# Statistics matmuls in a free column of the column transform's bank, and mixing pieces and head steps behind layer 3 dealt anew

## The chip, the cores and the metric

The kernel runs on one core of one Trainium2 chip. The metric is the device time of one execution in microseconds (us); lower is better. Runs are compared by their medians.

The engines are called by the profile's names: PE is the matmul engine (PEld its weight loads), DVE the vector engine, ACT the activation engine, POOL and SP the two that issue DMAs here. Results of matmuls land in PSUM, the accumulation memory, whose unit is a bank of 512 fp32 columns.

## The reference: what is computed

Eight images of 8 channels in 4 groups, 256 x 256 pixels each, go through two residual stages:

```python
x = x + _L0_conv_ref(_gn(x), ...)     # a spectral network
x = x + _L1_conv_ref(_gn(x))          # 3x3 dilation
```

`_gn` takes mean and variance of every group of an image and normalises by them. The spectral network lifts each group to 10 channels (fc0), and then four layers follow, each the sum of a spectral convolution (2D FFT, 12 x 12 low modes at two corners mixed by weights, inverse FFT) and of a 1x1 convolution. After each of the first three layers stands a gated activation. A head (fc1 to 128 channels per group, the activation, fc2 back to 2 channels per group) ends the network. The dilation is a 3x3 maximum with a border of -2; it needs mean and variance of the *whole* finished first stage before it can scale its result.

## The kernel before, in words

**Tiling.** An image's state `h` stays in SBUF as 11 chunks (`NCH`). Transforms are matmuls with cosine and sine tables; all is fp32.

**PSUM.** All eight banks are taken by two kinds of tiles: `ps_a` (L59) gives one bank, kind "one", two buffers; `ps_tri` (L62) gives three banks, kind "tri", two buffers. `ps_four` (L65) takes one of each, which makes four banks. A new tile of a kind goes to the older of the two buffers, and its first writer waits until the last reader of the tile there has ended.

**Order of the work.** PE, DVE, ACT and SP run in the order in which the program writes their instructions (`tc.manual_schedule`, L919). The order is dealt by hand: the generator `layers` (L691) writes image b's four layers and yields short strings, and for each letter the loop at L926 puts in other work:

- "f" is `first()` (L803), an f step: fc1 for a block of pixels of the image before, 4 products into a `ps_four` (8 matmul rows in the trace, L813), then two activations on ACT (L814, L815). A head has 128, f0 to f127. Every third or so first issues a load of `hs`, the stored state, on SP (`load_state`, L784).
- "c" is `second()` (L818), a c step: fc2 for two f steps (16 matmul rows, L830) into a "one" tile `acc`, which DVE then adds to `y` (L837 or L839). A head has 64, c0 to c63. With "c" the add is written at once; with "C" it is left until the next "f" or "c".
- "t" is `tail()` (L914), one step of the dilation of the image whose head has ended (`dilate`, L859).

Besides, layer 3 calls `next(side)` (L502, L612, L615), and each call writes one piece of the *next* image's preparation, the generator `start` (L673): `spectrum_x` (L265: its statistics and spectrum), then `mix` for layer 0 (L403: twelve pieces n0 to n11 on DVE, L411 and L414 in turn, the sums `fs` L432, and the folding matmuls `p_f`, L455 and L464, with DVE copies after them). What is left of it when layer 3 is over is written by `rest` (L680), between groups of head steps that the table `REST` (L43) lists:

```python
REST = ("ff", "f", "f", "fC", "fc"), ("f", "fc", "ffC", "ff", "fc")
...
        for n, _ in enumerate(then):
            yield REST[b > 0][n]
            for _ in range(2 if b == 0 else 1):
                if c < NCH:
                    read_x(b + 1, c)
                    c += 1
```

The first list is for image 0, the second for the others. `read_x(b + 1, c)` (L529) issues four SP DMAs that bring chunk c of the next image into `h`; behind image 0 all eleven are issued in `rest`, behind the others chunks 7 to 10 (chunks 0 to 6 are issued in layer 3, L621).

Counting the letters: the head of image b-1 ends (c63) in the `rest` behind image b, where f0 and on of image b's own head begin. Behind images 1 to 6 the order before is, with the last pieces of layer 3 in front,

```
burst 10, f126, c62, n4 n5, n6 n7, read 6 | n8 | f127 | read 7 | n9 | f0 c63 | read 8 | n10 |
f1 f2 C0 | read 9 | n11 | f3 f4 | read 10 | fs | f5 c1 | p_f and copies | f6 f7 c2 | p_g ...
```

**The finished image's statistics.** The tail begins with `stats_end` (L223). It joins the collected moments (L225, DVE), sums the means over a group's partitions by a matmul with `grp` (L229), takes them off (L231 to L234, DVE), sums the variances by a second matmul (L238) and ends in a reciprocal root on DVE (L242 and `rsqrt`, L248). Both matmuls have one output column, and each takes a "tri" tile of its own. The tail's first call lies in layer 0 of the image after (b = 2 to 7); the third lies behind `transform(0)` there, and the fifth behind `transform(1)`. The tail of image 6 and that of image 7 run in the drain at the end of the program (L946 to L953).

**The column transform.** `transform(k)` (L548), in layers 0 to 2: 64 matmuls (L558) into a `ps_four` named `p_d`, of which at most 480 of each bank's 512 columns are used; then DVE copies the "one" bank (L561) and ACT the three others (L562). In layer 0 there follow on PE a `burst` (L580, tiles `p_z`, L587 and L593, ended by ACT at L598) and, two steps later, `gather` (L564).

Of the kernel before, what the change touches and what calls it, by code (L numbers as in the profile page):

```python
# [13 lines left out]
ALU = mybir.AluOpType  # L14
# [25 lines left out]
DR = 2  # L40
STEPS = 128
BEHIND = mybir.DependencyInfo(mybir.DependencyClass.Sync, mybir.DependencyReason.DATA)
REST = ("ff", "f", "f", "fC", "fc"), ("f", "fc", "ffC", "ff", "fc")  # L43


@with_exitstack
def fno_dilate_kernel(ctx: ExitStack, tc: tile.TileContext, a: dict, out: bass.AP):
# [14 lines left out]
    def ps_tri(name):  # L62
        return ps.tile([128, 3, 512], F32, tag="tri", bufs=2, name=name)
# [5 lines left out]
    def part(i):  # L69
        return slice(32 * i, 32 * i + 32)  # L70
# [139 lines left out]
    def copy_banks(pairs, by_act):  # L210

        done = []
        for i, (dst, src) in enumerate(pairs):
# [6 lines left out]
                    tc.declare_no_dep(ins, other, reason="two engines read banks of one tile and write apart")  # L220
            done.append(ins)

    def stats_end(st, name, out_):  # L223
        mv = sb.tile([128, 2], F32, tag="mv", name=f"mv_{name}")
        nc.vector.bn_aggr(mv, st.rearrange("p n s -> p (n s)"))  # L225
        yield
        yield
        p = ps_tri(f"p_st_{name}")[:, 0, :]
        mm(p[:, 0:1], grp, mv[:, 0:1], start=True, stop=True)  # L229
        mr = sb.tile([128, 2], F32, tag="mr", bufs=4, name=f"mr_{name}")  # L230
        nc.vector.tensor_copy(mr[:, 0:1], p[:, 0:1])  # L231
        d = sb.tile([128, 1], F32, tag="d", name=f"d_{name}")
        nc.vector.tensor_tensor(d, mv[:, 0:1], mr[:, 0:1], ALU.subtract)
        nc.vector.scalar_tensor_tensor(mv[:, 1:2], d, d, mv[:, 1:2], ALU.mult, ALU.add)  # L234
        yield
        yield
        q = ps_tri(f"p_sv_{name}")[:, 0, :]
        mm(q[:, 0:1], grp, mv[:, 1:2], start=True, stop=True)  # L238


        v, r = mv[:, 0:1], mr[:, 1:2]
        nc.vector.tensor_scalar(v, q[:, 0:1], EPS, None, ALU.add)  # L242
        rsqrt(v, r, d)
        yield
        out_["mr"] = mr
# [19 lines left out]
    def spectrum_x(b, out_):  # L265

        x = turned[:, 0:2].rearrange("p i (g f) -> p i g f", g=G)
        st = sb.tile([128, G, 2, 6], F32, tag="bn", bufs=1, name=f"bn_x{b}")
        for i in range(2):
            for g in range(G):  # L270
                nc.vector.bn_stats(st[:, g, i, :], x[:, i, g])
            yield
        mv = sb.tile([128, G, 2], F32, tag="mvx", name=f"mv_x{b}")
        for g in range(G):
            nc.vector.bn_aggr(mv[:, g], st[:, g].rearrange("p n s -> p (n s)"))
        yield
        yield
        yield
        p = ps_a(f"p_st_x{b}")
        group_means(p, mv[:, :, 0])  # L280
        mr = sb.tile([128, 2, G + 1], F32, tag="mrx", name=f"mr_x{b}")
        d = sb.tile([128, 2, G + 1], F32, tag="dx", bufs=1, name=f"d_x{b}")
        nc.vector.tensor_copy(mr[:, 0], p[:, : G + 1])
        dm = d[:, 0, :G]
        nc.vector.tensor_tensor(dm, mv[:, :, 0], mr[:, 0, :G], ALU.subtract)
        nc.vector.tensor_tensor(dm, dm, dm, ALU.mult)
        nc.vector.tensor_tensor(dm, dm, mv[:, :, 1], ALU.add)
        yield
        yield
        q = ps_a(f"p_sv_x{b}")  # L290
        group_means(q, dm)
        nc.vector.tensor_scalar(d[:, 1], q[:, : G + 1], EPS, None, ALU.add)
        rsqrt(d[:, 1], mr[:, 1], d[:, 0])
        out_["mr"] = mr[:, :, G]
        for g in range(G):
            nc.vector.tensor_scalar(
                x[:, :, g], x[:, :, g], mr[:, 0, g : g + 1], mr[:, 1, g : g + 1], ALU.subtract, ALU.mult)
            if g != 1:
                yield
        yield  # L300

        a1, a2 = turned[:, 2, 0:512], turned[:, 2, 512:1024]
        a3 = turned[:, 2, 1024:1216].rearrange("p (g m) -> p g m", g=G)
        nc.vector.memset(a3, 0.0)
        p = ps_a(f"p_a1_{b}")
        for i in range(2):
            for g in range(G):
                mm(p[part(g)], er[:, i, :], x[:, i, g], start=i == 0, stop=i == 1)
        nc.vector.tensor_copy(a1, p)
        yield  # L310
        yield
        t = ps_a(f"p_a2_{b}")
        for i in range(4):
            nc.tensor.transpose(t[:, 128 * i : 128 * (i + 1)], a1[:, 128 * i : 128 * (i + 1)], ident)
        nc.vector.tensor_copy(a2, t)
        yield
        yield
        p = ps_a(f"p_a3_{b}")
        for j in range(2):
            for i in range(2):  # L320
                mm(p[:, 24 * j : 24 * j + 24], a2[:, 256 * j + 128 * i : 256 * j + 128 * i + 128], fw[:, i, 0:24],
                   start=i == 0, stop=i == 1)
        for g in range(G):
            nc.vector.tensor_copy(a3[part(g), g, :], p[part(g), 0:48])
        yield
        yield
        cols = a3.rearrange("p g (j k) -> p g j k", j=2)
        p = ps_a(f"p_xs_{b}")
        for k in range(2):
            for term in range(2):  # L330
                for q in range(4):
                    k0 = 12 * term + 3 * q
                    mm(p[part(q), 24 * k : 24 * k + 24], unf[:, spectrum_table(k, term), :],
                       cols[:, :, :, k0 : k0 + 3], start=term == 0, stop=term == 1)
        xe4 = xe.rearrange("p (s k) g j -> p s g j k", s=2)
        for k in range(2):
            nc.vector.tensor_copy(
                xe4[:, k, :, 0:2, :],
                p[:, 24 * k : 24 * k + 24].rearrange("p (g j k) -> p g j k", g=G, j=2),
            )  # L340
        yield
        bt = sb.tile([128, 2, 3, G, WID], F32, tag="B", bufs=1, name=f"B_{b}_0")
        prod = turned[:, 0, :1200].rearrange("p (i g o j) -> p i g o j", i=6, g=G, o=WID)
        for i in range(6):
            nc.vector.tensor_tensor(
                prod[:, i], wext, xe[:, i].unsqueeze(2).to_broadcast([128, G, WID, 5]), ALU.mult
            )
        nc.vector.tensor_reduce(
            bt.rearrange("p s k g o -> p (s k g o)"),
            prod.rearrange("p i g o j -> p (i g o) j"), AX.X, ALU.add,  # L350
        )
        out_["bt"] = bt
        yield
        yield

    def spectrum_table(k, term):

# [45 lines left out]
    def mix(b, l, out_):  # L403
# [3 lines left out]
        for n in range(12):  # L407
            k, k2 = n // 4, n // 2 % 2
            pr = turned[:, 2, 1024 * k2 : 1024 * k2 + 800].rearrange("p (g m i) -> p g m i", g=G, i=WID)
            if n % 2 == 0:  # L410
                nc.vector.tensor_tensor(  # L411
                    pr, sw[k], bt[:, k2, k].unsqueeze(2).to_broadcast([128, G, 2 * WID, WID]), ALU.mult)
            else:
                nc.vector.tensor_reduce(  # L414
                    s[k2][:, k].rearrange("p s o g -> p (s o) g"),
                    pr.rearrange("p g m i -> p m g i"), AX.X, ALU.add,
                )
            if l == 0:
                if n % 2 or n > 7:
                    yield  # L420
            elif n not in (0, 2, 6, 10):
                yield {1: "fc", 4: "fC", 7: "fC", 9: "fC"}.get(n, "f")
            if n == 2 and l == 3 and b + 1 < n_img:
                load_x(b + 1)
# [109 lines left out]
    def layer(b, l, out_, stored, side, ahead):  # L534
# [13 lines left out]
        def transform(k):  # L548


            cs = chunks_of(k)
            n, lo = len(cs), cs[0] % 3
            step = cs[-1] % 3 - lo if n == 2 else 1
            t = turned[:, lo : lo + step * (n - 1) + 1 : step].rearrange("p n (r v i) -> p n r v i", r=2 * NQ, v=8)
            one, tri, banks = ps_four(f"p_d_{b}_{l}_{k}")
            for v in range(8):
                for q in range(NQ):
                    mm(banks[q][part(v % 4), : 240 * n], fw8[part(q), v, :],  # L558
                       t[part(q), :, :, v, : NBLK * WID], start=v < 4, stop=v >= 4)
            e = turned[:, (2 * k + 1) % 3, : 960 * n].rearrange("p (q x) -> p q x", q=NQ)  # L560
            nc.vector.tensor_copy(e[:, 0], one[:, : 240 * n])  # L561
            nc.scalar.activation(e[:, 1:4], tri[:, :, : 240 * n], AF.Identity)  # L562
# [116 lines left out]

    def rest(b, then):  # L680
        c = 0 if b == 0 else NCH - 4
        for n, _ in enumerate(then):
            yield REST[b > 0][n]
            for _ in range(2 if b == 0 else 1):
                if c < NCH:
                    read_x(b + 1, c)
                    c += 1
        for i in range(c, NCH):
            read_x(b + 1, i)

    def layers(b, stored, d, then, ahead):  # L691

# [431 lines left out]
```

## Time and profile before

| what | us |
|---|---|
| median of 3 runs (3689.13 to 3691.84) | 3690.49 |
| the profiled execution | 3688.73 |
| its span, first to last instruction | 3687.0 |
| PE busy in the span | 3486.2 |
| ACT busy | 2865.0 |
| DVE busy | 2386.8 |
| from one `p_f` (L464) to the next, images 1 to 7 | 433.4, 438.7, 439.5, 436.8, 437.8, 438.5 |

The times in the table's upper part come from runs without and with the profiler; the rows below belong to the profiled execution alone. In the timelines, a row is a run of like instructions: start, length, engine, line, output and inputs, the count, and in brackets how long the engine had been idle before and what ended that. The ends of matmuls are modelled, so the start of the next row is the safer mark. Matmul rows count two for each fp32 product.

### The profile page before, as it was taken

To read this page: it belongs to the slowest core of one execution; us is meant where nothing else is said; L and a number is where in the kernel's file an instruction comes from. 1 tells how busy PE (TensorE), PEld (TensorE's weight loads), DVE (VectorE), ACT (ScalarE), POOL (GpSimd) and SP (SyncE) were. 2 spreads that over 40 slices of the span, in tenths; PEclk is the share of its full clock that TensorE was granted. 3 is DMA by queue.
4 is the path that set the end of the run, shared out by engine and by line. 5 is a ranking of instruction groups with operands and counts; after the bars stand their busy time and mean duration, and the time that the engine had idled before them with its cause. 6 is when DMAs were issued, how large, how long until landed. Compare 5 with 4: busy or idle time off the path is not lost.

```text
span 3687.0 us, 112658 instructions
## 1 busy us (share of the span) xinstructions
PE 3486.2 (95%) x50872; PEld 1270.1 (34%) x50872; DVE 2386.8 (65%) x3711; ACT 2865.0 (78%) x3021; POOL 117.1 (3%) x202
## 2 busy tenths in 40 slices
PE   5768999999999999999999999999999999999997
PEld 2323333333333333333333333333333333333222
DVE  6776666557775677757776577765777567772443
ACT  2436888888788788787888888888888888889986
POOL 1000000000000000000000000000000000000000
PEclk7879999999999999999999999999999999999998
DMA  3005111532226212271224512253222521225221
GB/s 92 16 17 212 49 50 46 165 106 72 72 84 195 68 58 72 87 226 53 65 57 138 170 55 75 64 168 114 67 73 89 189 75 58 71 65 193 84 82 48
DMA packets 114080, 344.71 MB, mean 93 GB/s; under 512 B 15984, under 2 KB 18480, under 8 KB 98176
## 3 DMA queue, kind: packets, MB, share of 16 engines
q1 hardware_dynamic: 95392, 276.32, 24.5%
q0 software_dynamic: 18208, 61.18, 5.1%
q8 instruction: 400, 6.55, 0.7%
q14 instruction: 80, 0.66, 0.1%
HBM read 213.44 MB, written 123.74 MB: 91 GB/s over the span
## 4 chain that ended last, share of the span: by engine, by line
PE 73%; DVE 16%; issue 5%; ACT 4%; DMA 2%; POOL 0%; ACTq 0%; DVEq 0%; POOLq 0%
PE p_fc L830 20%; PE p_fc L813 19%; PE p_z L593 9%; PE p_d L558 7%; PE p_z L590 7%; PE p_z L587 3%; DVE y L839 3%; PE p_u L572 3%; DVE turned L541 3%; DVE S L414 3%; DVE turned L411 2%; DMA yin<-y_rows 2%; DVE turned L372 1%; PE p_b L381 1%; PE p_g L509 1%
## 5 line engine op out<-in xcount | busy, mean ns | idle before, releaser
L815 ACT ACTIVATE act<-p_fc 128x1536 f32<-128x1536 f32 x1024 | 1493.2, 1458 | 0.0
L813 PE MATMUL p_fc<-hs,c_w 32*128 32x512 f32 x8192 | 1133.4, 625 | 41.2 <-DVE y L839 20.8
L830 PE MATMUL p_fc<-act,c_w 128*32 128x512 f32 x8192 | 1007.0, 600 | 0.2 <-ACT act L815 0.2
L814 ACT ACTIVATE act<-p_fc 128x512 f32<-128x512 f32 x1024 | 616.6, 602 | 228.2 <-PE p_fc L813 216.8
L541 DVE STREAM_TRANSPOSE turned<-h 128x1024 f32<-128x1024 f32 x528 | 632.6, 1226 | 189.7 <-ACT h L598 189.0
L598 ACT ACTIVATE h<-p_z 128x512 f32<-128x512 f32 (+1 forms) x528 | 511.9, 1021 | 213.9 <-PE p_z L593 213.9
L839 DVE TENSOR_TENSOR y<-p_fc,y 128x512 f32<-128x512 f32 x392 | 267.9, 684 | 539.1 <-PE p_fc L830 539.1
L813 PEld LDWEIGHTS p_fc<-hs,c_w 32*128 32x128 f32 x8192 | 358.3, 183 | 613.4 <-ACT act L814 253.3
L830 PEld LDWEIGHTS p_fc<-act,c_w 128*32 128x32 f32 x8192 | 221.4, 109 | 703.9 <-issue 330.8
L593 PE MATMUL p_z<-c_binv,zt 32*128 32x256 f32 x5632 | 410.3, 405 | 0.0
L590 PE MATMUL p_z<-h,c_wt 32*32 32x512 f32 x8448 | 357.8, 601 | 7.9 <-ACT act L814 4.2
L593 PEld LDWEIGHTS p_z<-c_binv,zt 32*128 32x128 f32 x5632 | 258.9, 186 | 308.0 <-issue 295.1
L558 PE MATMUL p_d<-turned,c_fw 32*32 32x480 f32 (+1 forms) x9216 | 307.6, 539 | 0.6 <-DVE turned L541 0.2
L562 ACT ACTIVATE turned<-p_d 128x1440 f32<-128x1440 f32 x144 | 183.0, 1271 | 89.5 <-PE p_d L558 86.3
L600 ACT ACTIVATE h<-p_z,c_bias 128x512 f32<-128x512 f32 (+1 forms) x176 | 186.4, 1110 | 72.0 <-PE p_z L593 71.8
L215 ACT ACTIVATE zt<-p_g 128x198 f32<-128x198 f32 (+2 forms) x118 | 53.4, 575 | 182.7 <-PE p_g L487 99.9
L414 DVE TENSOR_REDUCE S<-turned 128x80 f32<-128x800 f32 x192 | 189.0, 984 | 5.9
L411 DVE TENSOR_TENSOR turned<-t,B 128x800 f32<-128x800 f32 x192 | 188.7, 983 | 0.9
L558 PEld LDWEIGHTS p_d<-turned,c_fw 32*32 32x32 f32 x9216 | 127.1, 103 | 165.6 <-issue 64.7
L372 DVE STREAM_TRANSPOSE turned<-zt 128x960 f32<-128x960 f32 x96 | 176.8, 1867 | 2.5
L590 PEld LDWEIGHTS p_z<-h,c_wt 32*32 32x32 f32 x8448 | 92.9, 103 | 175.3 <-DVE y L839 48.8
L572 PE MATMUL p_u<-turned,c_stack 128*32 128x480 f32 (+1 forms) x1152 | 136.7, 543 | 11.5 <-DVE turned L561 6.2
(192 smaller groups left out, 1763.1 us busy)
## 6 DMA issues: line engine op xcount, KB each, us to landing
stored<-h SPq DMA_DIRECT2D x88, 1024.0 KB
hs<-stored SPq DMA_DIRECT2D x352, 256.0 KB
t<-in_spw SPq DMA_DIRECT2D x96, 400.0 KB
yin<-y_rows POOLq DMA_DIRECT2D x56, 512.0 KB, 5.2
h<-in_xp SPq DMA_DIRECT2D x352, 48.0 KB
turned<-in_xw SPq DMA_DIRECT2D x16, 1024.0 KB
y<-in_x SPq DMA_DIRECT2D x56, 256.0 KB
y_rows<-y POOLq DMA_DIRECT2D x56, 256.0 KB, 4.0
```

Source lines behind the costliest of these rows:

```text
L411: nc.vector.tensor_tensor(pr, sw[k], bt[:, k2, k].unsqueeze(2).to_broadcast([128, G, 2 * WID, WID]), ALU.mult)
L414: nc.vector.tensor_reduce(s[k2][:, k].rearrange("p s o g -> p (s o) g"), pr.rearrange("p g m i -> p m g i"), AX.X, ALU.add,)
L541: nc.vector.transpose(dst[:, 2 * i : 2 * i + 2], h[:, c, 2 * i : 2 * i + 2].rearrange("p f (s x) -> p f s x", s=2))
L558: mm(banks[q][part(v % 4), : 240 * n], fw8[part(q), v, :], t[part(q), :, :, v, : NBLK * WID], start=v < 4, stop=v >= 4)
L590: mm(o, wt[part(q), l, g, :], h[part(q), c, f, :], start=True, stop=False)
L593: mm(banks[q][:, HW * s : HW * (s + 1)], zt[part(q), 2 * c + s].rearrange("p f o -> p (f o)"), binv[part(q), :], start=False, stop=s == 1)
L598: nc.scalar.activation(dst, src, AF.Silu)
L813: mm(banks[g], w1[part(g), blk, :], hs[k][part(g), :], start=True, stop=True)
L814: nc.scalar.activation(act[:, 0, :], one, AF.Silu)
L815: nc.scalar.activation(act[:, 1:4, :], tri, AF.Silu)
L830: mm(acc[part(g), :], w2[:, g, 15 - rb - i : 47 - rb - i], act[:, g, :], start=i == 0, stop=i == 1)
L839: nc.vector.tensor_tensor(y, sums, y, ALU.add)
```

## The change

It has two parts.

**The statistics matmuls.** In layer 0, `transform(0)` and `transform(1)` now call `tail()` themselves, between their matmuls and the copies L561 and L562, if a tail is waiting. During that call the transform's "one" tile is set as `guest`, and `stats_end` puts its matmul's single column into column 511 of that tile, in place of a "tri" tile. Two added yields in `stats_end` make up for the two added calls, so the DVE instructions of the tail stay at the calls at which they stood.

**Dealing.** `spectrum_x` loses one of two yields at its end, and layer 0's `mix` yields after every second piece to the end, not after every piece from n8 on. That leaves three calls for `rest` in place of six. `REST` has three groups for each list, and four chunks are read per group. The order behind images 1 to 6 becomes

```
burst 8, ..., f123, n0 n1 | burst 9, f124, c61, n2 n3, f125, n4 n5 | burst 10, f126, c62, n6 n7, n8 n9, read 6 |
f127 f0 c63 | reads 7 8 9 10 | n10 n11 | f1 f2 | fs | C0 f3 f4 c1 f5 | p_f and copies | f6 f7 c2 | p_g ...
```

where before n0 to n3 stood with burst 9 and n4 to n7 with burst 10. Behind image 0 the head steps keep their order (f0 to f4, C0, f5, c1), and the reads are dealt 4, 4, 3 in place of 2, 2, 2, 2, 2, 1. Behind image 7 `rest` returns at once.

```diff
-REST = ("ff", "f", "f", "fC", "fc"), ("f", "fc", "ffC", "ff", "fc")
+REST = ("fff", "ff", "Cfc"), ("ffc", "ff", "Cffcf")
...
+    guest = [None]
+
+    def corner(name):
+
+        return ps_tri(name)[:, 0, 0:1] if guest[0] is None else guest[0][:, 511:512]
+
     def stats_end(st, name, out_):
...
-        p = ps_tri(f"p_st_{name}")[:, 0, :]
-        mm(p[:, 0:1], grp, mv[:, 0:1], start=True, stop=True)
+        p = corner(f"p_st_{name}")
+        mm(p, grp, mv[:, 0:1], start=True, stop=True)
+        if guest[0] is not None:
+            yield
         mr = sb.tile([128, 2], F32, tag="mr", bufs=4, name=f"mr_{name}")
-        nc.vector.tensor_copy(mr[:, 0:1], p[:, 0:1])
+        nc.vector.tensor_copy(mr[:, 0:1], p)
...
-        q = ps_tri(f"p_sv_{name}")[:, 0, :]
-        mm(q[:, 0:1], grp, mv[:, 1:2], start=True, stop=True)
+        q = corner(f"p_sv_{name}")
+        mm(q, grp, mv[:, 1:2], start=True, stop=True)
+        if guest[0] is not None:
+            yield
...
-        nc.vector.tensor_scalar(v, q[:, 0:1], EPS, None, ALU.add)
+        nc.vector.tensor_scalar(v, q, EPS, None, ALU.add)
...
         out_["bt"] = bt
         yield
-        yield
...
             if l == 0:
-                if n % 2 or n > 7:
+                if n % 2:
                     yield
...
+            if l == 0 and k < 2 and tails:
+                guest[0] = one
+                tail()
+                guest[0] = None
             e = turned[:, (2 * k + 1) % 3, : 960 * n].rearrange("p (q x) -> p q x", q=NQ)
...
     def rest(b, then):
         c = 0 if b == 0 else NCH - 4
-        for n, _ in enumerate(then):
+        if b + 1 == n_img:
+            return
+        for n in range(3):
             yield REST[b > 0][n]
-            for _ in range(2 if b == 0 else 1):
-                if c < NCH:
-                    read_x(b + 1, c)
-                    c += 1
-        for i in range(c, NCH):
-            read_x(b + 1, i)
+            for i in range(c + 4 * n, min(c + 4 * n + 4, NCH)):
+                read_x(b + 1, i)
+            next(then, None)
```

## The prediction, on record before the result

> **What bounds the kernel now.** I read the page first:
>
> ```profile
> PE 3486.2 (95%) x50872; PEld 1270.1 (34%) x50872; DVE 2386.8 (65%) x3711; ACT 2865.0 (78%) x3021; POOL 117.1 (3%) x202
> ...
> PE 73%; DVE 16%; issue 5%; ACT 4%; DMA 2%; POOL 0%; ACTq 0%; DVEq 0%; POOLq 0%
> ```
>
> PE is busy 95% of the span and holds 73% of the chain that ended last; most of its idle 200 us lie in image 0's stretch, ahead of 340 us. So a gain has to be taken out of PE's own timeline: rows that vanish, and gaps or stretched rows. I therefore read PE's timeline at the two places that the diff touches. Behind layer 3 of image 1 (f127 starts at 760.30):
>
> ```profile
> 760.30 2.47 PE L813 MATMUL p_fc<-hs,c_w 32*128 32x512 f32 x16
> ...
> 764.56 1.14 PE L813 MATMUL p_fc<-hs,c_w 32*128 32x512 f32 x8
> 767.51 1.14 PE L813 MATMUL p_fc<-hs,c_w 32*128 32x512 f32 x8 [1.81 <-DVE y L839]
> ...
> 770.43 2.93 PE L813 MATMUL p_fc<-hs,c_w 32*128 32x512 f32 x18
> 773.58 1.13 PE L813 MATMUL p_fc<-hs,c_w 32*128 32x512 f32 x6 [0.22 <-ACT act L815]
> ...
> 776.50 0.88 PE L455 MATMUL p_f<-fs,c_fold 32*32 32x72 f32 x64
> ...
> 781.49 0.73 PE L487 MATMUL p_g<-c_rowg,fz 32*128 32x264 f32 x8
> ```
>
> The reader is to see two losses. f2 waits 1.81 us for the add of c63. And f3, f4, f5 stand in a row: 24 matmul rows take 770.43 to 774.64, 4.21 us, where three free groups of eight take 3 x 1.07 = 3.21 (764.56 to 765.63 is one). DVE's timeline says why f2 waits: c63 ended on PE at 764.56, but two mixing pieces written ahead of its add were still in DVE's queue:
>
> ```profile
> 764.85 0.98 DVE L411 TENSOR_TENSOR turned<-t,B 128x800 f32<-128x800 f32 x1
> 765.87 0.99 DVE L414 TENSOR_REDUCE S<-turned 128x80 f32<-128x800 f32 x1
> 766.77 0.68 DVE L839 TENSOR_TENSOR y<-p_fc,y 128x512 f32<-128x512 f32 x1
> ```
>
> The 1.81 recurs behind images 2 to 6. The second place is `transform(0)` in layer 0, in image 2 with a tail and in image 1 without one:
>
> ```profile
> 798.79 2.24 PE L558 MATMUL p_d<-turned,c_fw 32*32 32x480 f32 x64
> 800.96 0.38 PE L229 MATMUL p_st_y<-mv_y,c_grp 128*128 128x1 f32 x2
> 801.27 1.74 PE L587 MATMUL p_z<-h,wcn 6*32 6x512 f32 x32
> 802.95 1.15 PE L593 MATMUL p_z<-c_binv,zt 32*128 32x256 f32 x16
> ...
> 365.38 2.19 PE L558 MATMUL p_d<-turned,c_fw 32*32 32x480 f32 x61
> ...
> 368.61 1.15 PE L593 MATMUL p_z<-c_binv,zt 32*128 32x256 f32 x16
> ```
>
> From the start of the transform to the burst's L593 it takes 4.16 us with the statistics and 3.23 without: 0.93. The same for `transform(1)`: 812.23 to 816.43 against 377.88 to 381.16, 4.20 against 3.28, 0.92. Only 0.31 of it is the matmul itself (800.96 to 801.27); the rest is the burst, whose L587 rows are stretched to 1.74, since the small matmul's "tri" tile turned the rotation: the burst's three banks are now those that the transform has just filled, and ACT's copy of them (L562) takes 1.37 us. The granted clock was 1.00 in both stretches.
>
> **What the skill says.** PSUM — Partial Sum Buffer, Specifications: eight banks of 512 fp32 values per partition; the kernel's tiles take all eight, so a statistics matmul can only borrow. The trace agrees as far as it shows the burst wait. The same page, "PSUM bank collisions raise a hardware error": a matmul must not write a bank and quadrant that another engine reads, so that accesses are to be guarded by bank. Here it means that the copy L561 has to come after the statistics matmul; no run here shows a collision. TensorE: Matmul & The Clock Gate, Part 1: the clock is set to 4/8 after a slack window of about 3.4 us. The trace agrees: behind image 1 it has stretches of 3.41 us at half clock, at 1206.1 (3 us after such a 1.81 wait) and at 1230.0.
>
> **The change part by part.** *Statistics matmuls* (images 2 to 7, six times). Removed: two "tri" tiles per image, thus the turned rotation. The burst then takes the three banks of the burst before, which ACT frees at 800.82 (798.88 + 1.94), before PE wants them. Remaining: the matmul, 0.31 each. So 0.93 + 0.92 - 2 x 0.31 = **1.2 us per image**. Bounds: 0.9, if the 128-row matmul cannot begin under the transform's tail as the burst's first rows do now (367.01 against 367.45), to 1.3. Added waits: the copy L561 stands behind the matmul, 0.3 us later; behind it on DVE are the tail's three short operations and two transposes, and DVE then idles 1.49 us, so nobody is late. If that cover went, the cost would be 0.3. The "one" bank stays taken until L231 (801.67) or L242 (815.15); its next users are f12 at 803.91 and f15 at 817.40. The matmul waits for L225, done at 788.1. POOL's DMAs of the tail stand at the same calls. Images 1 and 0 have no tail there, and the drain's two tails take the old way: nothing.
>
> *Dealing, behind images 1 to 6.* Four pieces, n6 to n9, lie on DVE from 761.01 to 764.85, then c63's add at once: it ends at 765.54, where it ended at 767.45. f1 ends at 765.63, so f2's wait is gone. I follow PE on: f2 to 766.70; C0 needs f1's activation, which ends at 767.66, halfway through it: to 768.65; f3 to 769.72; f4 needs the add of C0, on DVE behind n10, n11 and `fs` (766.2 + 1.94 + 0.87 = 769.0, then 0.75): 0.1 wait, to 770.88; c1 to 772.73 (1.85); f5 to 773.80; `p_f` to 775.0 (1.21); f6 waits for f5's activation, some 0.1, then f6, f7 and c2 (2.14 + 1.85, with 0.1 for that wait) to 779.1. `p_g` stood at 781.49: **2.3 us per image**. Of it 1.85 is the add and the rest is c1 between f4 and f5, so that ACT, which takes 1.82 per f step (759.65 to 761.46), isn't fed three in a row. Bounds: below, 0.9, if ACT falls behind at f5 to f7 and only half of the wait is kept; above 2.9, the bare sum of the rows.
>
> The pieces that come earlier, n0 to n5, go into DVE's idle time ahead of the adds of c61 and c62 (2.45 us and 1.71 us idle there): n0 and n1 end at 753.7, and c61 is due at 754.17; n2 to n5 run 754.78 to 758.7, and c62 is due at 760.41. Nothing, while that cover holds; without it up to 1.9 per pair of pieces. Their data (`sw`, `bt`) were there at 751.7.
>
> *Reads.* SP takes them in this order before:
>
> ```profile
> 760.48 5.23 SPq L532 DMA_DIRECT2D h<-in_xp  x8
> 766.49 0.35 SPq L789 DMA_DIRECT2D hs<-stored  x1
> 767.07 4.89 SPq L532 DMA_DIRECT2D h<-in_xp  x8
> 772.30 0.35 SPq L789 DMA_DIRECT2D hs<-stored  x1
> ```
>
> After, state 3 (f0) goes ahead of read 7, and reads 7 to 10, 16 issues at some 0.63, stand ahead of state 4 (f3): at about 774, 2 us later. It is first used by f12 at 803.9. Read 10 waits for chunk 10's store, issued at 759.79, and comes at about 771. Chunks 7 to 10 are read by bursts after 820. Nothing. POOL's queue gets c63's row write 1.9 earlier, and its first `yin` load with it. Behind image 0 the head steps and SP's order (state 3, reads 0 to 3, state 4, the rest) are the same, and DVE's pieces run without a break in both: nothing.
>
> Sum: 6 x 1.2 + 6 x 2.3 = 7.2 + 13.8 = 21.0. Span 3687.0 - 21.0 = 3666.0; profiled execution 3667.7; the median of the runs stands 1.8 above it: **3669.5**.
>
> **Rivals.** *A, both parts as worked*: 3669.5; with the upper bounds of both, 6 x 4.2 = 25, it is 3665; downward it reaches halfway to B, 3674. *B, ACT takes the wait's place*: after the dealing f1 to f7 come closer together, and ACT has 1.82 of every f step. For it: f127 and f0 are already stretched (2.47 for two). Against: nine f steps are 16.4 us of ACT in about 19 of PE. Then the dealing gives 0.9 and the sum is 6 x 2.1 = 12.6: 3678. *C, the dealing gives nothing*, for another add becomes as late as c63's was, or the program's order isn't what I counted: 6 x 1.1: 3684. *D, slower: DVE becomes the bound at layer 3's end.* If the earlier pieces hold up the adds of c61, c62 and c63 by a pair each, PE waits up to 3 x 1.94 = 5.8 per image, and 6 x (5.8 - 1.2) = 28 more: 3718. It decides from 2.4 per image: 7.4 over six, and the 1.2 of the statistics; the dealing's gain is gone with the late adds. Against: the idle DVE shown. Half-clock stretches cost 1.7 each: one fewer or one more moves any of these.
>
> **How the numbers follow.** A 0.67, B 0.16, C 0.10, D 0.07. A measurement of this kernel tells some 0.2% from no change: 7.4 us, 3683.1 to 3697.9. A and B are faster: 0.83; C is the same: 0.10; D slower: 0.07. The range runs from A with its upper bounds and two half-clock stretches fewer (3690.5 - 25 - 3.4 = 3662) to C: 3661 to 3684.
>
> **What would show it.** Right: L229 starts about 2.2 us behind the transform, L587 there takes 1.2 and not 1.74, and 3.55 us pass from transform to L593; f2 shows no wait for L839; no row of three f steps; `p_g` 18.8 to 19.5 us behind f127's start (21.19 before); from `p_f` to `p_f` about 434. Wrong: c61's or c62's add late behind mixing pieces, waits for L815 at f5 or f6, L229 waiting, or a late state load ahead of f12.

## The result and the profile after

| | median, us | lowest to highest |
|---|---|---|
| before, 5 runs | 3690.49 | 3689.13 to 3693.64 |
| after, 5 runs | 3671.2 | 3669.93 to 3671.84 |

The ratio is 0.9944, with a 95% interval of 0.9931 to 0.9957: 19.3 us less. The prediction said 3669.5, and 21.0 less. The profiled execution took 3669.94, and its span is 18.9 us shorter than before.

The page after, the line of busy times and that of the chain:

```profile
PE 3478.0 (95%) x50872; PEld 1269.3 (35%) x50872; DVE 2388.5 (65%) x3711; ACT 2865.8 (78%) x3021; POOL 117.0 (3%) x202
...
PE 74%; DVE 15%; issue 5%; ACT 4%; DMA 2%; POOL 0%; ACTq 0%; DVEq 0%; POOLq 0%
```

They hardly differ from before: same instructions, same bound. 18.9 us in 3687 can't be read from shares. PE's timeline at the two places can. Behind layer 3 of image 1, after (f127 starts at 759.59; line numbers have moved, L825 is fc1, L842 fc2, L464 `p_f`, L496 `p_g`):

```profile
763.85 2.17 PE L825 MATMUL p_fc<-hs,c_w 32*128 32x512 f32 x16
...
767.99 2.25 PE L825 MATMUL p_fc<-hs,c_w 32*128 32x512 f32 x16
...
772.12 1.14 PE L825 MATMUL p_fc<-hs,c_w 32*128 32x512 f32 x8
773.20 0.88 PE L464 MATMUL p_f<-fs,c_fold 32*32 32x72 f32 x64
...
774.19 3.08 PE L825 MATMUL p_fc<-hs,c_w 32*128 32x512 f32 x16
777.20 1.92 PE L842 MATMUL p_fc<-act,c_w 128*32 128x512 f32 x16
779.05 0.73 PE L496 MATMUL p_g<-c_rowg,fz 32*128 32x264 f32 x8
```

f1 and f2 now stand in one row without a wait, and f3, f4 are no longer stretched by f5. But f6 and f7 take 3.08 us where they took 2.00: a new stretch. From f127 to `p_g` it is 19.46 (779.05 - 759.59), where it was 21.19. The same 19.46 stands behind each of images 1 to 6; before it was 21.19 in five of them and 22.84 behind image 2. The new stretch hides inside a row: the profile counts PE as busy for all of the 19.46 us. DVE's row for c63's add (L851), after:

```profile
763.24 0.99 DVE L423 TENSOR_REDUCE S<-turned 128x80 f32<-128x800 f32 x1
764.14 0.68 DVE L851 TENSOR_TENSOR y<-p_fc,y 128x512 f32<-128x512 f32 x1
```

The add starts 4.55 us behind f127's start; before, it was 6.47 (766.77 - 760.30). ACT's rows for f5 and f6, after, show where the new stretch comes from:

```profile
773.28 0.60 ACT L826 ACTIVATE act<-p_fc 128x512 f32<-128x512 f32 x1 [0.36 <-PE p_fc L825]
773.78 1.45 ACT L827 ACTIVATE act<-p_fc 128x1536 f32<-128x1536 f32 x1
775.35 0.60 ACT L826 ACTIVATE act<-p_fc 128x512 f32<-128x512 f32 x1
776.47 1.45 ACT L827 ACTIVATE act<-p_fc 128x1536 f32<-128x1536 f32 x1 [0.52 <-PE p_fc L825]
```

f5's rows begin on PE at 772.12, but its first activation starts only at 773.28, when the whole step has ended (773.20), and the second ends at 775.23. Between f5 and f6 lies `p_f`, which takes the other "tri" buffer, so f6 needs the buffer that f5's activation holds until then. The profile's list of waits names it too: between 774 and 777.5 PEld, f6's weight loads, waits 0.8 us for L827. In layer 0 of image 2, after (L235 is the first statistics matmul, now into `p_d`):

```profile
796.34 2.24 PE L567 MATMUL p_d<-turned,c_fw 32*32 32x480 f32 x64
798.51 0.38 PE L235 MATMUL p_d<-mv_y,c_grp 128*128 128x1 f32 x2
798.83 1.14 PE L600 MATMUL p_z<-h,wcn 6*32 6x512 f32 x32
799.90 1.16 PE L606 MATMUL p_z<-c_binv,zt 32*128 32x256 f32 x16
```

The burst's first rows take 1.14, not 1.74, and from transform to L606 it is 3.56; behind `transform(1)` 3.60. DVE's copy of the bank (L574) starts at 798.93, behind the statistics matmul. Both repeat in images 2 to 7.

The difference of the two profiles by place: 6 x 1.73 = 10.4 in the dealing, 6 x 1.15 = 6.9 in layer 0 from burst 0 to `p_b` (78.91 to 78.99 before, 77.77 to 77.82 after, in the images in which no stretch at half clock, a granted clock of 0.50, falls there), and 1.65 of one stretch at half clock behind image 2 that after doesn't have. That is 18.95 of the 18.9; image 0's start (0.84 less), the images' way from `p_b` to the next f127 (0.71 more) and all that follows the last of these places (0.22 more) about cancel.

### The profile page after: what moved, and what is told of

It reads as the page before. It is cut to its first block, busy times and chain, and to the rows that moved or that the text cites. A ratio compares the mean times of both kernels' runs of the same rounds, so it can differ in the third digit from the quotient of the medians.

```text
span 3668.1 us, 112640 instructions
## 1 busy us (share of the span) xinstructions
PE 3478.0 (95%) x50872; PEld 1269.3 (35%) x50872; DVE 2388.5 (65%) x3711; ACT 2865.8 (78%) x3021; POOL 117.0 (3%) x202
## 4 chain that ended last, share of the span: by engine, by line
PE 74%; DVE 15%; issue 5%; ACT 4%; DMA 2%; POOL 0%; ACTq 0%; DVEq 0%; POOLq 0%
PE p_fc L842 20%; PE p_fc L825 20%; PE p_z L606 9%; PE p_d L567 7%; PE p_z L603 7%; PE p_z L600 3%; DVE turned L550 3%; PE p_u L585 3%; DVE y L851 3%; DVE S L423 2%; DVE turned L420 2%; DMA yin<-y_rows 2%; DVE turned L381 1%; PE p_g L518 1%; PE p_b L390 1%
## 5 line engine op out<-in xcount | busy, mean ns | idle before, releaser
L827 ACT ACTIVATE act<-p_fc 128x1536 f32<-128x1536 f32 x1024 | 1493.0, 1458 | 3.1 <-PE p_fc L825 3.1
L825 PE MATMUL p_fc<-hs,c_w 32*128 32x512 f32 x8192 | 1133.3, 626 | 29.8 <-DVE y L851 10.0
L842 PE MATMUL p_fc<-act,c_w 128*32 128x512 f32 x8192 | 1007.5, 599 | 0.2 <-ACT act L827 0.2
L851 DVE TENSOR_TENSOR y<-p_fc,y 128x512 f32<-128x512 f32 x392 | 267.9, 683 | 524.9 <-PE p_fc L842 524.9
L825 PEld LDWEIGHTS p_fc<-hs,c_w 32*128 32x128 f32 x8192 | 356.6, 183 | 602.0 <-ACT act L826 259.2
L842 PEld LDWEIGHTS p_fc<-act,c_w 128*32 128x32 f32 x8192 | 222.5, 109 | 704.7 <-issue 330.7
L606 PE MATMUL p_z<-c_binv,zt 32*128 32x256 f32 x5632 | 410.4, 405 | 0.0
L606 PEld LDWEIGHTS p_z<-c_binv,zt 32*128 32x128 f32 x5632 | 259.3, 186 | 307.5 <-issue 294.4
```

The source lines that it names most:

```text
L606: mm(banks[q][:, HW * s : HW * (s + 1)], zt[part(q), 2 * c + s].rearrange("p f o -> p (f o)"), binv[part(q), :], start=False, stop=s == 1)
L825: mm(banks[g], w1[part(g), blk, :], hs[k][part(g), :], start=True, stop=True)
L827: nc.scalar.activation(act[:, 1:4, :], tri, AF.Silu)
L842: mm(acc[part(g), :], w2[:, g, 15 - rb - i : 47 - rb - i], act[:, g, :], start=i == 0, stop=i == 1)
L851: nc.vector.tensor_tensor(y, sums, y, ALU.add)
```

## The experiments

The theory was that the two parts are independent and that each acts at its one place on PE; the rivals were that one part does it all, that the reads have a share, and, for the statistics, that the size of the tile counts and not the turned rotation. "Before" was run again beside each set, with medians of 3690.1 to 3691.4.

**The parts alone.** e1 has the statistics in the transform's bank and the old dealing; e2 has the new dealing, and `transform` doesn't call the tail:

```diff
-            if l == 0 and k < 2 and tails:
-                guest[0] = one
-                tail()
-                guest[0] = None
```

> The statistics matmuls in the transform's bank, with the old dealing. Theory (the two parts are independent and add up; the statistics give 1.15 us in each of six images): 6.9 us less than before, about 3683.6; from transform to the burst's second set of matmuls 3.56 and 3.60, as after; the wait of 1.81 ahead of f2 stays. Rival (the gain comes from the dealing alone, or the statistics' gain is taken back by the next wait): 3690, no change.

> The new dealing, with the statistics matmuls in tiles of their own. Theory: 6 x 1.73 = 10.4 us less than before, about 3680, or 1.7 less again if a stretch at half clock falls away; 19.46 us from f127 to the row matmuls. Rival (one part needs the other): less than half of that.

e1: 3683.81, ratio 0.9982 (0.9975 to 0.9988), 6.4 less. f2's wait is still there (first line), and the burst is as after (the others):

```profile
2085.46 1.14 PE L827 MATMUL p_fc<-hs,c_w 32*128 32x512 f32 x8 [1.80 <-DVE y L853]
...
2116.75 2.24 PE L568 MATMUL p_d<-turned,c_fw 32*32 32x480 f32 x64
...
2119.23 1.14 PE L601 MATMUL p_z<-h,wcn 6*32 6x512 f32 x32
2120.30 1.16 PE L607 MATMUL p_z<-c_binv,zt 32*128 32x256 f32 x16
```

e2: 3676.87, ratio 0.997 (0.9958 to 0.9981), 13.3 less; 19.46 behind every image, and bursts at 4.16 and 4.21. The parts add: 6.4 + 13.3 = 19.7 against 19.3. The dealing brought more than the 10.4 of its places; the last part of this section takes that up.

**c1 ahead of f5.** The prediction gave this exchange some 0.45 per image. e3 makes it in the kernel before, e4 undoes it in the kernel after:

```diff
-REST = ("ff", "f", "f", "fC", "fc"), ("f", "fc", "ffC", "ff", "fc")
+REST = ("ff", "f", "f", "fC", "fc"), ("f", "fc", "ffC", "ff", "cf")
```
```diff
-REST = ("fff", "ff", "Cfc"), ("ffc", "ff", "Cffcf")
+REST = ("fff", "ff", "Cfc"), ("ffc", "ff", "Cfffc")
```

> The kernel before with one exchange: c1 ahead of f5 in the group behind layer 3, pieces and reads as before. The prediction's step (c1 between f4 and f5 keeps ACT from three f steps in a row): 0.45 us in each of six images, 2.7 less, about 3687.8. Theory now (the exchange moves ACT's wait from f5 to f6 and gains nothing, since f6 then follows f5 with only the folding matmuls between): 3690.5, within 1 us; 21.2 us from f127 to the row matmuls, with f6 and f7 taking 3.1 and not 2.0.

> The kernel after with c1 put back behind f5. Theory now: no change against after, 3671 within 1 us, with f3 to f5 stretched again and f6, f7 at 2.0. The prediction's step: 2.7 more, about 3674.

e3: 3691.6, ratio 1.0006 (0.9998 to 1.0014). e4: 3672.15, ratio to before 0.9956 (0.9943 to 0.9968), against 0.9944 for after. From f127 to `p_g` e3 has 21.20 and e4 has 19.46. In e4 the row of three f steps is back, and f6, f7 are free:

```profile
769.19 4.28 PE L825 MATMUL p_fc<-hs,c_w 32*128 32x512 f32 x24
...
776.46 2.00 PE L825 MATMUL p_fc<-hs,c_w 32*128 32x512 f32 x16
```

Here three f steps take 4.28 and the two behind `p_f` 2.00; in after f3 and f4 take 2.25, f5 1.14, and the two behind `p_f` 3.08. From f127 to `p_g` the two orders are equal, so the exchange gains nothing in either kernel: the wait moves from f5 to f6. Of the medians, e3's rules out the 2.7 (its interval allows 0.7 less at most); e4's can't (11.8 to 21.0 less than before), and there the 19.46 decides. e3 says a second thing: it has after's order of head steps, but the old places of pieces and reads, and none of the gain.

**f5 behind the folding matmuls**, to see whether the wait can be got rid of by one more move:

```diff
-REST = ("fff", "ff", "Cfc"), ("ffc", "ff", "Cffcf")
+REST = ("fff", "ff", "Cfc"), ("ffc", "ff", "Cffc")
...
-        yield "ffc"
+        yield "ffcf" if l == 0 and b > 1 else "ffc"
```

> The kernel after with f5 moved behind the folding matmuls (f3 f4 c1, folding, f5 f6 c2 f7, row matmuls, f8). Theory (a tile of three banks comes free only 1.95 us after its f step, so of three users in a row of the two buffers the third waits unless a c step lies between; the user pair f7, row matmuls, f8 then has none): f6's wait of 1.1 us goes, f8 gets one of about as much, 3671 within 1.5 us; f127 to the row matmuls 18.6, row matmuls to burst 0 longer by about 0.9. Rival (the wait belongs to f5 and the folding matmuls alone): 6 x 0.9 = 5.4 less than after, 3666.

3671.39, ratio to before 0.9956 (0.9944 to 0.9968): no gain on after is seen. From f127 to `p_g` it is 18.89 (0.57 less), and from `p_g` to burst 0 it is 7.06 (0.60 more). The wait now stands at f8:

```profile
778.34 0.64 PE L496 MATMUL p_g<-c_rowg,fz 32*128 32x264 f32 x8
779.19 1.12 PE L825 MATMUL p_fc<-hs,c_w 32*128 32x512 f32 x2 [0.21 <-ACT act L826]
780.53 0.70 PE L825 MATMUL p_fc<-hs,c_w 32*128 32x512 f32 x3 [0.22 <-ACT act L827]
```

One rival stays untested. In after ACT is busy 17.62 of the 19.46 us from f127 to `p_g`, so ACT's load alone leaves any order little to gain. How much of the 19.46 is due to that load, and how much to there being only two buffers, was not separated.

**The reads.** e6 is after, with chunks 7 to 10 read one by one, behind f127, c63, f2 and f4:

```diff
-            yield REST[b > 0][n]
-            for i in range(c + 4 * n, min(c + 4 * n + 4, NCH)):
-                read_x(b + 1, i)
+            if b == 0:
+                yield REST[0][n]
+                for i in range(4 * n, min(4 * n + 4, NCH)):
+                    read_x(1, i)
+            else:
+                for j, kind in enumerate(REST[1][n]):
+                    yield kind
+                    if (n, j) in ((0, 0), (0, 2), (1, 1), (2, 2)):
+                        read_x(b + 1, c)
+                        c += 1
```

> The kernel after with the reads of chunks 7 to 10 dealt one by one again between the head steps, pieces and steps as after. Theory (the reads cost nothing in either place): 3671 within 1 us and 19.46 from f127 to the row matmuls. Rival (part of the gain comes from the reads): between 3674 and 3680.

3670.35, ratio 0.9952 (0.994 to 0.9964), and 19.46 behind every image, as in after: the reads have no share there. With e3 this leaves the pieces.

**The pieces by dose.** e8 is the kernel before, with f0 and c63 moved ahead of n9 alone, so that DVE has five pieces ahead of the add where before had six and after four:

```diff
-REST = ("ff", "f", "f", "fC", "fc"), ("f", "fc", "ffC", "ff", "fc")
+REST = ("ff", "f", "f", "fC", "fc"), ("ffc", "f", "fC", "ff", "fc")
```

> The kernel before with only f0 and c63 moved ahead of mixing piece n9, so that five pieces and not six stand ahead of c63's add. Theory (the gain is the add's place in DVE's order, piece by piece): f2 waits some 0.85 us in place of 1.81, 20.2 us from f127 to the row matmuls, 5.7 us less than before. If the long wait is also what brings the stretches at half clock right behind it (9 of 24 such places in the profiles with the old dealing, 0 of 30 with the new), there are none here and some 3 us more go: 3681 to 3684. Rival (the reads or the fewer, larger groups bring the gain): 3690.

3681.73, ratio 0.9974 (0.9963 to 0.9984), 9.7 less than the 3691.42 beside it. f2's wait:

```profile
766.84 1.14 PE L813 MATMUL p_fc<-hs,c_w 32*128 32x512 f32 x8 [0.79 <-DVE y L839]
```

From f127 to `p_g` it is 20.17, so 1.02 less per image and 6.1 in all. The remaining 3.6 fit the half clock. In the four profiles with the 1.81 wait (before, e1, e3, e7) 9 of 24 places have a stretch of 3.41 us at half clock, which costs 1.65, and each begins 7.2 to 8.8 us behind f127's start, at or just behind the wait's end (7.2). In e8 it is none of 6, and in the five profiles with the new dealing none of 30. 9/24 of six images at 1.65 is 3.7 per execution: with it the dealing is worth 10.4 + 3.7 = 14.1 (e2 measured 13.3), and e8 6.1 + 3.7 = 9.8 (9.7 measured). Two of before's windows, the 3.4 us ahead of such a stretch and the stretch itself (columns: length, busy PE, PEld, DVE, ACT and POOL, granted clock, DMA share, GB/s):

```profile
1206.10:1209.50 3.40, 3.40 (x20) 0.92 (x16) 1.59 (x3) 1.62 (x2) 0.00 (x0) 0.50 0.55 146
1202.70:1206.10 3.40, 1.59 (x18) 0.48 (x18) 3.33 (x5) 2.26 (x3) 0.54 (x1) 1.00 0.58 128
```

PE was busy 1.59 of 3.40 us ahead of it. That the wait brings the half clock is supported by the counts, by e8 and by where the stretches begin (last section); no edit changed the clock alone.

**A bank of its own.** e7 is before with the statistics matmuls in tiles of one bank:

```diff
-        p = ps_tri(f"p_st_{name}")[:, 0, :]
+        p = ps_a(f"p_st_{name}")
...
-        q = ps_tri(f"p_sv_{name}")[:, 0, :]
+        q = ps_a(f"p_sv_{name}")
```

> The kernel before with the statistics matmuls in a tile of one bank in place of three. Theory (it is the turn of the rotation that stretches the burst, whichever kind of tile turns; the burst's first bank then is the one that DVE copies, free some 3.0 us behind the transform's start): about 4.1 us from transform to the burst's second set in place of 4.16, 3690 within 1 us. Rival (it is the size of the tile, or ACT's slow copy): 3.6 as in the shared bank, 3683.6.

From transform to L593 it is 4.17 and 4.22: as long as with three banks, and the wait now names DVE's copy of the transform's first bank.

```profile
801.49 0.38 PE L229 MATMUL p_st_y<-mv_y,c_grp 128*128 128x1 f32 x2
802.31 1.25 PE L587 MATMUL p_z<-h,wcn 6*32 6x512 f32 x32 [0.44 <-DVE turned L561]
```

So it is the turn of the rotation. The median of 3694.43 (ratio 1.0014, 1.0007 to 1.002) is 4 us above before, though; its profiled span, 3690.7, has stretches as long as before's in layer 0 and behind layer 3, and no single place shows the 4 us. That stays open.

## Why the prediction was right, and where a term was off

- *Statistics, 1.2 per image:* 1.15 measured in the profile; 6.4 alone against 7.2. The stretched burst was the turned rotation (e7), the rest of 0.31 each stays, and the copy waits behind the matmul (798.93, against the matmul's start at 798.51) at no cost. In these six images no statistics matmul waited for the joined moments.
- *c63's add, 1.85 per image:* f2's wait of 1.81 is gone, and e8 gives 1.02 of it for one piece.
- *"the rest is c1 between f4 and f5", 0.45 of the 2.3:* failed. The working's times have f5's activation begin under f5's own rows and f6 wait "some 0.1". The activation begins only when all of the f step is through, and `p_f` uses up a "tri" buffer, so f6 and f7 took 3.01 from start to start (774.19 to 777.20) in place of 2.14 + 0.1. Of the prediction's own signs of being wrong, a wait for L815 at f6 thus came true. The dealing was worth 1.73 at its place, not 2.3: 3.4 us too much over six. (The steps of the working add up to 2.4, 781.49 less 779.1; 2.3 was carried on.) Rival B's mechanism, ACT in the wait's place, was thus at work, though it took 0.6 and not 1.4.
- *Half clock:* I left it outside the sum, as one more or less. By the counts the wait had drawn it: about 3.7 per execution, which makes up for the 3.4. With it the parts add up to 6.9 + 10.4 + 3.7 = 21.0. That this is the predicted sum again is luck: two terms were off in opposite directions. The measured 19.3, with an interval of 15.9 to 25.5, is too wide to check the account to 2 us.
- *Pieces ahead of c61 and c62:* DVE still waits for PE ahead of those adds, 0.40 and 1.71 us, so rival D had no ground; but 0.40 is thin cover.
- *Reads:* state 3 went ahead of read 7, the 16 issues took 10.99 us, and state 4 came at 773.78, as the working had it at "about 774":

```profile
762.29 0.35 SPq L801 DMA_DIRECT2D hs<-stored  x1
762.69 10.99 SPq L541 DMA_DIRECT2D h<-in_xp  x16
773.78 7.70 SPq L801 DMA_DIRECT2D hs<-stored  x3
```

## What to carry to other kernels

With an order written by hand, look for what stands *ahead of a release* on an engine that has time: two pieces of 0.98 us ahead of one add cost the bound engine 1.81 us. A small result that takes a buffer of a rotation costs more than its matmul (here 0.93 us against 0.31), since the next user gets the younger buffer; in a free column of a tile that is about to be read anyway it cost little more than the matmul (0.33, 3.56 against 3.23). And where two buffers serve steps whose release takes longer than the next step (1.95 us for an f step's two activations here, 773.28 to 775.23, against 1.07 for the step's rows), exchanging neighbours can move the wait in place of removing it, as it did here (21.20 against 21.19, 19.46 against 19.46); count the work between each user and the one after the next.

## What was unexpected in the hardware

A pause of 1.81 us in 3.4 us was enough for a stretch at half clock in 9 of 24 places, and one of 0.79 in none of 6. The Trainium skill (TensorE: Matmul & The Clock Gate, Part 1) speaks of a free-running window of 3413 ns, and of half clock after at least one idle window. The traces agree on the window: in each of the ten profiles all switches of the clock lie on one grid with a step of 3.413 us. They differ on the idleness: PE was busy 1.59 of the 3.40 us ahead of 1206.1. A pause doesn't have to fill the window. The prediction overlooked this where it said that the trace agreed, and it put the stretch 3 us after the wait; it begins 1.5 us after the wait's end (1206.10 against 1204.56).

How the grid falls decides much of it. In 12 of the 24 places one window of the grid held the whole pause (5.4 to 7.2 us behind f127's start), and 9 of these windows were followed by half clock; in the other 12 the grid cut the pause in two, and none was. Why three were spared is open. In e8 only two windows held all of the 0.79, so its none of 6 is thin by itself.

Half-clock stretches also begin 3.2 to 3.9 us behind the start of layer 0's first burst in 17 of 60 places of the ten profiles, before and after the change alike, and there PE's rows leave no gap (3.40 busy of 3.40 us ahead of the one at 1658.3 in after). These 17 are all the places in which a window of the grid ended between 3.21 and 3.88 us behind that start; windows that ended at 3.19 and 3.95 brought none. Two thirds of the matmul rows there have weights of 6 rows only (32 of 48 in a burst). Whether that is the cause wasn't tried.
